# Layers 1 and 2 of a graph stack: rows gathered as plain fp32 and split on chip into two float32r pieces

## The chip, the cores and the metric

The kernel runs on one core of a Trainium2 chip. The metric is device time in microseconds (us) of the whole launch, as the median of several runs: 1704.35 us for the kernel before (three runs, 1702.13 to 1708.13). One more execution was taken by the hardware profiler; its times are those of the profile below. The engines are TensorE (PE, with its weight loads shown apart as PEld), VectorE (DVE), ScalarE (ACT), GpSimd (POOL) and SyncE (SP). Each runs its own instructions in order and waits on semaphores for the others.

## The reference

There are 3,327 nodes with 512 features each, and an adjacency matrix of 0 and 1 with some eight neighbours in the mean, but very many in the first rows. Four graph layers follow one another, each wrapped in a residual and a layer norm. What matters here are layers 1 and 2:

```python
# layer 1
mask = (adj > 0).astype(x.dtype)
deg = jnp.sum(mask, axis=1, keepdims=True)
agg = mask @ x / jnp.maximum(deg, 1.0)
self_f = x @ W_self + b_self
nb_f = agg @ W_nb + b_nb
out = relu(jnp.concatenate([self_f, nb_f], axis=-1) @ W_comb + b_comb)
x = layernorm(x + out)
# layer 2: the first 64 neighbours of each row are kept
nb_mean = keep @ x / jnp.maximum(cnt, 1.0)
out = leaky_relu(x @ W_line.T + b_line) + where(cnt > 0, leaky_relu(nb_mean @ W_nb.T + b_nb), 0)
x = layernorm(x + out)
```

Layers 0 and 3 are attention layers: every edge is weighted by a softmax over the row's neighbours, with 8 heads in layer 0 and 4 in layer 3.

## The kernel before

The nodes lie in 26 blocks of 128. From the adjacency matrix the kernel first makes, for every block, a list of its edges on chip (indices of the source rows and the place of the target row in the block), cut into chunks of 128 edges. Blocks 1 to 25 have 19 down to 5 chunks, 201 in all. Block 0, with the densest rows, is computed without a list: all 26 blocks of rows are read as they lie, and a 0/1 mask (`row0` in layer 1, `near0` in layer 2) takes the place of the selection.

Layers 1 and 2 share one routine, `mean_group` (L1452). The weights are applied first: the end of the layer before multiplies each block by the neighbour weights and stores the products in a table in DRAM, `t1_d` for layer 1 and `t2_d` for layer 2 (L727, L729). A row of a table holds three bf16 pieces of 512 values, whose sum is the fp32 value; `pieces` (L808) makes them with two ACT and two DVE instructions a block. `mean_group` works on groups of up to four chunks, in stages; at every `yield` it lets the other live groups and block ends go on:

1. `gather` (L962) takes slots of a ring in SBUF and issues on POOL one indirect DMA for each chunk (L966): 128 rows by index. For block 0 these are plain DMAs, also from POOL (L1460).
2. `select` (L975) has DVE compare the edge's place with the lane number. This gives a 128x128 matrix of 0 and 1 per chunk, in bf16 in layer 1; in layer 2 in fp8, into `sall`, which layer 3 uses again.
3. For every chunk PE multiplies the selection with the three pieces, three matmuls of 512 columns (L1474), all added up in one PSUM bank per block.

When a block's last group is done, its end is queued: `layer1_end` (L1512) and `layer2_end` (L1612) divide by the degree, add what the node itself gives, normalise, transpose the block, multiply it by the next layer's weights, and store the next table (L738, on SP). `layer0_end` (L1376) does the same at the end of layer 0 and fills `t1_d`. The function `both` (L1482) takes one step of every live group, oldest first, and then one step of every live block end, and is called once for every group; this order is how the instructions stand on each engine. It is written out by hand from L1430 on; the stages before may be put in another order.

The ring is laid out in two tiles, `gt` (22 x 528 fp32 columns, `RING`, L544) and `gx` (3,072 columns, `MORE`, L545), which hold 15 and 4 rows of 3,072 bytes. Layer 0 and layer 3 use the same tiles for their own rows. A gather waits until the matmuls that read its slots before are done. `first_block` in layer 3 (L1092) computes block 0 there, with four tiles `gd` of its own for the rows that it reads.

The loop of layer 1 adds, besides the groups, the products of the node's own rows (`self_part`, L1503, and `own_part`, L1539) as block ends, so that PE has them between the groups.

Of the kernel before, what the change touches and what calls it, by code (L numbers as in the profile page):

```python
# [8 lines left out]
F32 = mybir.dt.float32  # L9
BF16 = mybir.dt.bfloat16  # L10
FP8 = mybir.dt.float8e4
F32R = mybir.dt.float32r
# [6 lines left out]
ALU = mybir.AluOpType  # L19
# [524 lines left out]
RING = 22 * 528  # L544
MORE = 3072  # L545
RANGE = 60.0
# [75 lines left out]
def sparse_path(ctx, tc, flag_i, x, adj, l0_w, l0_a1, l0_a2, l1_w_self, l1_b_self, l1_w_nb, l1_b_nb,  # L622
# [103 lines left out]
    t0_d = dram.tile([ROWS, H0 * (OUT0 + 2)], F32, name="t0_d")  # L726
    t1_d = dram.tile([ROWS, 3 * D], BF16, name="t1_d")  # L727
    z1_d = dram.tile([NP, D], F32, name="z1_d")
    t2_d = dram.tile([ROWS, 3 * D], BF16, name="t2_d")  # L729
    t3_d = dram.tile([ROWS, H3 * (OUT3 + 2)], F32, name="t3_d")  # L730
# [252 lines left out]
    class Gat:  # L983
# [107 lines left out]

        def first_block(self, pool, ps, pacc, mp, none, done):  # L1092

# [13 lines left out]
            nc.scalar.copy(lone, pl[0:1, :P])  # L1107
            G = pool.tile([P, H, M], F32, name="gd", bufs=4)
            nc.sync.dma_start(G[0:1].rearrange("p h m -> p (h m)"), self.table[0:1, :])
# [6 lines left out]
            def unit(c):  # L1116
                m = LAST if c == NB - 1 else P
                G = pool.tile([P, H, M], F32, name="gd", bufs=4)
                nc.sync.dma_start(G[:m].rearrange("p h m -> p (h m)"), self.table[2 + c * P:2 + c * P + m, :])
# [124 lines left out]
    lay, listlay, wxlay = ExitStack(), ExitStack(), ExitStack()  # L1244
    rows = pool_in(ctx, "s_rows").tile([P, RING], F32, name="gt")
    big = pool_in(listlay, "l0big")
# [13 lines left out]
    with ExitStack() as pro:  # L1260
# [57 lines left out]
        def first_rows():  # L1318

            zeros16 = lent(3 * D, BF16)  # L1320
            nc.gpsimd.memset(zeros16, 0.0)
            zero = zeros16[0:1, :]
            for r in range(2):
# [128 lines left out]
    def mean_group(item, table, whole0, done, sall=None):  # L1452
        b, l, c0, g, at = item
        n = NB if b == 0 else chunks_of[b]
        if b == 0:
            G = ring.take(g)
            for c in range(g):
                m = LAST if c0 + c == NB - 1 else P
                r0 = 2 + (c0 + c) * P
                nc.gpsimd.dma_start(G[:m, c, :], table[r0:r0 + m, :])  # L1460
            S = whole0[:, c0:c0 + g, :]
            yield
        else:
            G = gather(ring, table, l, c0, g)
            yield
            S = select(sp, l.dst, c0, g, BF16, kept(sall, b, at, g))
        yield
        if at == 0:
            accs[b] = pacc.tile([P, D], F32, name="acc")
        for c in range(g):  # L1470

            m = LAST if b == 0 and c0 + c == NB - 1 else P if b == 0 or sall else l.places(c0 + c)
# [12 lines left out]

    ring = Ring(3 * D, rows.bitcast(BF16), extra.bitcast(BF16))
    mlay = ExitStack()
# [4 lines left out]
    with ExitStack() as lay:  # L1492
# [19 lines left out]
        def layer1_end(b, acc):  # L1512
# [63 lines left out]
    with ExitStack() as lay:  # L1576
# [57 lines left out]
        while work.live or ends.live:  # L1634
            both()
        assert not summed2
        g3.finish(fin, ps)
    mlay.close()

    with ExitStack() as lay:
        pools = (Ring(H3 * (OUT3 + 2), rows, extra), pool_in(lay, "l3s", 3),
                 pool_in(lay, "l3pa", 4, space=PSUM), pool_in(lay, "l3p1", 3, space=PSUM))
# [12 lines left out]
        def verdict():  # L1656
# [11 lines left out]
            for ls in lists:  # L1668
                for l in ls:
# [15 lines left out]
        units = g3.first_block(pool_in(lay, "l3d", 2), pools[3], pools[2], pool_in(lay, "l3pm", 1, space=PSUM),  # L1685
                               nl, layer3)
        dense = Stages()
# [60 lines left out]
```

## Time and profile before

| what | value |
|---|---|
| median of the runs | 1704.35 us |
| span of the profiled execution | 1704.1 us |
| PE busy | 1523.7 us (89%) |
| DVE busy | 1243.4 us (73%) |
| POOL busy | 911.9 us (54%) |
| ACT busy | 773.2 us (45%) |
| first and last matmul of `mean_group`, layer 1 | 650.5 and 1025.5 us |
| the same, layer 2 | 1031.7 and 1353.2 us |
| gathers by index (L966), all layers | 846 |
| DMA traffic | 410.17 MB, mean 241 GB/s |

The span is the time from the first to the last instruction of the one execution that was profiled; the page gives no other time for it. In the profile a group of instructions has its line of the code, engine and operation, the tiles that it writes and reads (out<-in), partitions x elements and type, and the count. Then come the time in which at least one of them ran, the mean of one in ns, and the idle time of the engine before them with what ended it. PE's instructions overlap, so the busy time over the count is what one of them costs in a row, and the mean is longer. POOL's busy time is the time that it takes to issue its DMAs; the transfers run on after it. An fp32 matmul stands in the trace as two instructions.

### The profile page before, as it was taken

Reading aid. Unit: us, or ns where it says so; the run is one execution under the profiler, and the core shown is the slowest. Engines: PE = TensorE matmul, PEld = TensorE weight load, DVE = VectorE, ACT = ScalarE, POOL = GpSimd, SP = SyncE. Lnnn points to the kernel's source line nnn. Section 1 sums busy time; section 2 is a strip of 40 time slices with the busy share of each in tenths; the row PEclk is TensorE's granted clock in tenths of the full one; section 3 lists DMA queues with packets and bytes.
Section 4 is the critical chain, followed back from the end, with each engine's and each line's share of the span. In section 5 each row is a group of like instructions: output and inputs, shape, how many; then the busy total and the mean of one; then the engine's idle time right before and its main releaser. Section 6 shows DMA issues by size and latency. Waiting matters only on the chain.

```text
span 1704.1 us, 25362 instructions
## 1 busy us (share of the span) xinstructions
PE 1523.7 (89%) x7947; PEld 981.5 (58%) x7947; DVE 1243.4 (73%) x3256; ACT 773.2 (45%) x2411; POOL 911.9 (54%) x1008
## 2 busy tenths in 40 slices
PE   5798958999999999999999999889989866998774
PEld 4565746777666664444444444446555545877653
DVE  8999988999998973124777884565434468798986
ACT  6557855667776764111111121122223222566664
POOL 2000067777666613646776552477777552677770
PEclk9999979999999999999999999999999987999997
DMA  8623687998775637978998776589999664677772
GB/s 300 233 100 107 207 288 237 313 309 266 258 231 176 179 90 282 317 237 272 341 328 296 246 241 241 204 279 317 318 312 322 234 227 157 189 230 224 227 220 74
DMA packets 121982, 410.17 MB, mean 241 GB/s; under 512 B 24768, under 2 KB 26304, under 8 KB 121838
## 3 DMA queue, kind: packets, MB, share of 16 engines
q0 software_dynamic: 69584, 286.13, 52.8%
q1 hardware_dynamic: 52254, 122.32, 20.4%
q8 instruction: 65, 1.06, 0.3%
q14 instruction: 79, 0.65, 0.1%
HBM read 360.34 MB, written 48.04 MB: 240 GB/s over the span
## 4 chain that ended last, share of the span: by engine, by line
PE 61%; DVE 16%; DMA 11%; ACT 6%; issue 3%; POOL 2%; SPq 0%; DVEq 0%; ACTq 0%; POOLq 0%
PE po L765 20%; PE acc L1196 15%; PE acc L1474 14%; DMA gt<-t_d,idx 7%; PE po L998 6%; PE pt L750 2%; DVE cand L877 2%; DVE gt L1188 2%; DMA gx<-t_d,idx 2%; POOL gt L966 2%; PE pg L1168 2%; DMA gd<-t_d 1%; DVE cand L891 1%; DVE sl L889 1%; ACT h L1213 1%
## 5 line engine op out<-in xcount | busy, mean ns | idle before, releaser
L966 POOL DMA_INDIRECT gt<-t_d,idx x739 | 742.1, 1004 | 578.9 <-DVE some L893 210.6
L1196 PE MATMUL acc<-gt,sel 128*128 128x264 f32 (+4 forms) x1656 | 413.7, 399 | 27.1 <-issue 20.1
L1196 PEld LDWEIGHTS acc<-gt,sel 128*128 128x128 f32 (+2 forms) x1656 | 311.4, 195 | 97.8 <-issue 42.9
L1188 DVE TENSOR_TENSOR gt<-gt,pg 128x1536 f32<-128x1536 f32 (+2 forms) x128 | 238.6, 1864 | 6.3 <-ACT gt L1181 2.9
L765 PE MATMUL po<-wn,xt 128*128 128x512 f32 x416 | 192.9, 607 | 3.8 <-ACT xt L753 3.8
L1474 PE MATMUL acc<-gt,sall 128*128 128x512 bf16 x489 | 117.3, 379 | 17.6 <-DMA gt<-t_d,idx 14.3
L765 PEld LDWEIGHTS po<-wn,xt 128*128 128x128 f32 x416 | 77.2, 193 | 89.4 <-issue 78.4
L966 POOL DMA_INDIRECT gx<-t_d,idx x107 | 107.6, 1006 | 38.6 <-issue 14.9
L877 DVE MAX8 cand<-val 128x8 f32<-128x832 uint16 (+38 forms) x259 | 125.7, 522 | 0.0
L1474 PEld LDWEIGHTS <-sall 128*128 128x128 fp8e4 x603 | 58.3, 97 | 98.4 <-issue 35.3
L1474 PE MATMUL acc<-gt,sel 128*128 128x512 bf16 (+3 forms) x486 | 113.3, 379 | 0.0
L998 PE MATMUL po<-gt,xt 128*128 128x268 f32 x416 | 106.0, 400 | 2.0 <-ACT xt L757 1.7
L1474 PEld LDWEIGHTS <-sel 128*128 128x128 bf16 (+3 forms) x603 | 57.9, 98 | 80.0 <-issue 22.7
L1156 ACT ACTIVATE far<-place,nmid 128x384 int16<-128x384 int16 (+3 forms) x137 | 86.9, 637 | 37.5 <-DVE ds L1160 34.5
L753 ACT COPY xt<-pt 128x512 f32<-128x512 f32 x86 | 50.8, 591 | 113.3 <-PE pt L750 113.2
L998 PE MATMUL po<-w,xt 128*128 128x262 f32 x416 | 96.2, 384 | 1.6 <-ACT xt L757 1.6
L765 PE MATMUL po<-wl,xt 128*128 128x512 f32 x208 | 94.0, 594 | 2.9 <-ACT xt L753 2.9
L765 PE MATMUL po<-wx,xt 128*128 128x512 f32 x208 | 94.3, 596 | 1.3 <-ACT xt L753 1.2
L750 PE MATMUL pt<-s_ident,xres 128*128 128x128 f32 x520 | 79.9, 277 | 17.4 <-DMA xres<-in_x_dram 16.6
L750 PEld LDWEIGHTS pt<-s_ident,xres 128*128 128x128 f32 x520 | 63.8, 143 | 46.2 <-issue 31.2
L1009 ACT COPY tg<-po 128x264 f32<-128x264 f32 (+1 forms) x104 | 39.9, 392 | 110.8 <-PE po L998 108.9
L849 ACT ACTIVATE m<-ab 128x1664 bf16<-128x1664 int32 x50 | 80.4, 1607 | 20.5 <-DMA ab<-in_adj_dram 15.6
(273 smaller groups left out, 2555.4 us busy)
## 6 DMA issues: line engine op xcount, KB each, us to landing
ab<-in_adj_dram SPq DMA_DIRECT2D x25, 832.0 KB
ab<-in_adj_dram SPq DMA_DIRECT2D x25, 831.5 KB
t_d<-t SPq DMA_DIRECT2D x50, 384.0 KB
gt<-t_d POOLq DMA_DIRECT2D x38, 384.0 KB, 7.8
gt<-t_d,idx POOLq DMA_INDIRECT x739, 4.8
t_d<-tg SPq DMA_DIRECT2D x25, 264.0 KB
t_d<-tg SPq DMA_DIRECT2D x25, 260.0 KB
gd<-t_d SPq DMA_DIRECT2D x25, 260.0 KB
```

Source lines behind the costliest of these rows:

```text
L750: nc.tensor.transpose(pt[:, c, :], src[:, c * P:(c + 1) * P], ident)
L753: nc.scalar.copy(xt, pt)
L765: nc.tensor.matmul(po, xt[:, c, :], w[:, c], start=c == 0, stop=c == DC - 1)
L849: nc.scalar.activation(m, ab[s], AF.Sign, accum_out=half[:, s, b:b + 1])
L877: nc.vector.max(out=top, in_=seg)
L966: nc.gpsimd.indirect_dma_start(out=t[:m, c, :], out_offset=None, in_=table[:, :], in_offset=bass.IndirectOffsetOnAxis(ap=l.idx[:m, c0 + c: ...
L998: nc.tensor.matmul(pw[s], xt[:, c, :], self.w[:, c, s, :], start=c == 0, stop=c == DC - 1)
L1009: nc.scalar.copy(tb[:, s * hh:(s + 1) * hh, :], by_head[:, :, 1:])
L1156: nc.scalar.activation(far[:, :g * P], place[:, c0 * P:(c0 + g) * P], AF.Abs, bias=l.nmid, scale=2.0)
L1188: nc.vector.tensor_mul(Gc[:, :, :OUT], Gc[:, :, :OUT], w[:, :g].rearrange("p c (h o) -> p (c h) o", o=1).to_broadcast([P, g * H, OUT]))
L1196: nc.tensor.matmul(accs[b][s], S[:m, c, :], G[:m, c, s * hh * M:(s + 1) * hh * M], start=at + c == 0, stop=at + c == chunks_of[b] - 1)
L1474: nc.tensor.matmul(accs[b], S[:m, c, :], G[:m, c, k * D:(k + 1) * D], start=at + c + k == 0, stop=k == 2 and at + c == n - 1)
```

## The change

The tables `t1_d` and `t2_d` hold plain fp32 rows, 2,048 bytes instead of 3,072. Where `pieces` made three bf16 pieces, layer 0's end copies the product from PSUM with one ACT instruction and stores it; layer 1's end stores its sum as it is. The split moves to the reader. `mean_group` has one stage more: ACT copies the gathered group into `hi`, a float32r tile (rounded), DVE subtracts `hi` from the gathered rows in place and leaves a float32r tile `lo`, and PE makes two matmuls for each chunk, with `hi` and `lo`. The selection is float32r too: in layer 1 DVE writes it so; in layer 2 DVE still writes fp8 into `sall`, and ACT converts it; for block 0 ACT converts the mask.

The buffers change with it. The ring of layers 1 and 2 is one tile `gm` on the place of `gt`, with 16 slots of 512 columns, and behind them the first of three `hi` tiles and the first of three selections. Two more `hi` tiles lie where `gx` lay and beside it. For layer 3 the place is given back as a new tile `gr`, and POOL fills it and `gx`, now 2,112 columns, with zeros. `first_block` takes its four row tiles from the second of the side tiles.

```diff
-MORE = 3072
+MEAN = 16
...
-    t1_d = dram.tile([ROWS, 3 * D], BF16, name="t1_d")
+    t1_d = dram.tile([ROWS, D], F32, name="t1_d")
...
-    t2_d = dram.tile([ROWS, 3 * D], BF16, name="t2_d")
+    t2_d = dram.tile([ROWS, D], F32, name="t2_d")
...
+            held = [t.rearrange("p (h m) -> p h m", m=M) for t in
+                    (room[:, q * H * M:(q + 1) * H * M] for q in range(GROUP))]
+            G = held[-1]
...
-                G = pool.tile([P, H, M], F32, name="gd", bufs=4)
+                G = held[c % GROUP]
...
         tb = fin.tile([P, D], F32, name="tb", bufs=2)
-        t3 = fin.tile([P, 3, D], BF16, name="t3", bufs=2)
-        for _ in pieces(t3, tb, times(ps, xt, wn)):
-            pass
-        store(t1_d, b, t3.rearrange("p s d -> p (s d)"), 2)
+        nc.scalar.copy(tb, times(ps, xt, wn))
+        store(t1_d, b, tb, 2)
...
-            extra = pool_in(ctx, "s_more").tile([P, MORE], F32, name="gx")
-            sp = pool_in(ctx, "s_sel", 3)
+            aside = pool_in(ctx, "s_more", 2)
+            for _ in range(2):
+                aside.tile([P, GROUP * H3 * (OUT3 + 2)], F32, name="gx", tag="aside")
+            sp = pool_in(ctx, "s_sel", 2)
...
-            S = whole0[:, c0:c0 + g, :]
-            yield
         else:
             G = gather(ring, table, l, c0, g)
-            yield
-            S = select(sp, l.dst, c0, g, BF16, kept(sall, b, at, g))
+        yield
+
+        S, hi = sels.pop(0), upper.pop(0)
+        sels.append(S)
+        upper.append(hi)
+        if b == 0:
+            nc.scalar.activation(S[:, :g], whole0[:, c0:c0 + g, :], AF.Identity)
+        elif sall is None:
+            nc.vector.tensor_tensor(S[:, :g], lane1[:, None, :].to_broadcast([P, g, P]),
+                                    l.dst[:, c0:c0 + g, None].to_broadcast([P, g, P]), ALU.is_equal)
+        else:
+            have = select(sp, l.dst, c0, g, BF16, kept(sall, b, at, g))
+            nc.scalar.activation(S[:, :g], have, AF.Identity)
+        nc.scalar.copy(hi[:, :g], G)
+        yield
+        lo = G.bitcast(F32R)
+        nc.vector.tensor_sub(lo, G, hi[:, :g].bitcast(F32))
         yield
...
-            for k in range(3):
-                nc.tensor.matmul(accs[b], S[:m, c, :], G[:m, c, k * D:(k + 1) * D],
-                                 start=at + c + k == 0, stop=k == 2 and at + c == n - 1)
+            m = l.places(c0 + c) if b else LAST if c0 + c == NB - 1 else P
+            for k, part in enumerate((hi, lo)):
+                nc.tensor.matmul(accs[b], S[:m, c, :], part[:m, c, :],
+                                 start=at + c + k == 0, stop=k == 1 and at + c == n - 1)
...
-    ring = Ring(3 * D, rows.bitcast(BF16), extra.bitcast(BF16))
+    gm = room.tile([P, RING], F32R, name="gm", tag="ring")
+    wide, narrow = GROUP * D, GROUP * P
+    ring = Ring(D, gm[:, :MEAN * D].bitcast(F32))
+    upper = [gm[:, MEAN * D:MEAN * D + wide]]
+    upper += [aside.tile([P, GROUP * H3 * (OUT3 + 2)], F32R, name="hi", tag="aside")[:, :wide] for _ in range(2)]
+    upper = [t.rearrange("p (c d) -> p c d", d=D) for t in upper]
+    sels = [gm[:, MEAN * D + wide:MEAN * D + wide + narrow].rearrange("p (c i) -> p c i", i=P)]
+    sels += [sp.tile([P, GROUP, P], F32R, name="selr") for _ in range(2)]
...
-            t3 = fin.tile([P, 3, D], BF16, name="t3")
...
-            yield from pieces(t3, tb)
-            store(t2_d, b, t3.rearrange("p s d -> p (s d)"), 2)
+            store(t2_d, b, tb, 2)
...
+        rows = room.tile([P, RING], F32, name="gr", tag="ring")
+        extra = [aside.tile([P, GROUP * H3 * (OUT3 + 2)], F32, name=name, tag="aside") for name in ("gx", "gd")]
+        for t in (rows, extra[0]):
+            nc.gpsimd.memset(t, 0.0)
         g3.finish(fin, ps)
```

More of the change, by code (lines that the diff above doesn't have):

```diff
@@ L1090, in factors, with first_block @@
             return wide
-        def first_block(self, pool, ps, pacc, mp, none, done):
+        def first_block(self, pool, ps, pacc, mp, none, done, room):
             H, OUT, M = self.H, self.OUT, self.M
@@ L1117, in unit @@
                 m = LAST if c == NB - 1 else P
-                G = pool.tile([P, H, M], F32, name="gd", bufs=4)
+                G = held[c % GROUP]
                 nc.sync.dma_start(G[:m].rearrange("p h m -> p (h m)"), self.table[2 + c * P:2 + c * P + m, :])
@@ L1244, in sparse_path @@
     lay, listlay, wxlay = ExitStack(), ExitStack(), ExitStack()
-    rows = pool_in(ctx, "s_rows").tile([P, RING], F32, name="gt")
+    room = pool_in(ctx, "s_rows")
+    rows = room.tile([P, RING], F32, name="gt", tag="ring")
     big = pool_in(listlay, "l0big")
@@ L1318, in first_rows @@
         def first_rows():
-            zeros16 = lent(3 * D, BF16)
-            nc.gpsimd.memset(zeros16, 0.0)
-            zero = zeros16[0:1, :]
+            blank = lent(D)
+            nc.gpsimd.memset(blank, 0.0)
+            zero = blank[0:1, :]
             for r in range(2):
@@ L1470, in mean_group @@
         for c in range(g):
-            m = LAST if b == 0 and c0 + c == NB - 1 else P if b == 0 or sall else l.places(c0 + c)
-            for k in range(3):
-                nc.tensor.matmul(accs[b], S[:m, c, :], G[:m, c, k * D:(k + 1) * D],
-                                 start=at + c + k == 0, stop=k == 2 and at + c == n - 1)
+            m = l.places(c0 + c) if b else LAST if c0 + c == NB - 1 else P
+            for k, part in enumerate((hi, lo)):
+                nc.tensor.matmul(accs[b], S[:m, c, :], part[:m, c, :],
+                                 start=at + c + k == 0, stop=k == 1 and at + c == n - 1)
         ring.done()
@@ L1641, in sparse_path @@
     with ExitStack() as lay:
-        pools = (Ring(H3 * (OUT3 + 2), rows, extra), pool_in(lay, "l3s", 3),
+        pools = (Ring(H3 * (OUT3 + 2), rows, extra[0]), pool_in(lay, "l3s", 3),
                  pool_in(lay, "l3pa", 4, space=PSUM), pool_in(lay, "l3p1", 3, space=PSUM))
@@ L1685, in sparse_path @@
         units = g3.first_block(pool_in(lay, "l3d", 2), pools[3], pools[2], pool_in(lay, "l3pm", 1, space=PSUM),
-                               nl, layer3)
+                               nl, layer3, extra[1])
         dense = Stages()
```

## The prediction

> **What bounds the kernel now.** I read the page's slices first, to cut the span at the stages; then the busy time in those stretches, the waits, the chain, the groups by shape and the timeline. These stretches carry layer 1 (642 to 1100 us), layer 2 (1100 to 1353) and, for comparison, the middle of layer 3:
>
> ```profile
> core 0: us, PE busy (x) PEld busy (x) DVE busy (x) ACT busy (x) POOL busy (x), PEclk, DMA share, GB/s
> ...
> 712.00:800.00 88.00, 88.00 (x318) 41.39 (x317) 28.06 (x55) 16.84 (x31) 45.66 (x48) 1.00 0.76 248
> 800.00:1025.00 225.00, 224.38 (x800) 102.35 (x799) 173.28 (x357) 41.20 (x80) 146.01 (x147) 1.00 0.87 293
> 1025.00:1100.00 75.00, 68.89 (x234) 32.76 (x232) 34.77 (x60) 13.55 (x29) 21.51 (x28) 1.00 0.56 202
> 1100.00:1353.00 253.00, 228.55 (x1062) 138.81 (x1063) 127.00 (x312) 66.24 (x326) 191.03 (x189) 1.00 0.91 310
> 1500.00:1600.00 100.00, 86.37 (x594) 71.05 (x593) 90.39 (x207) 63.25 (x188) 76.22 (x79) 1.00 0.78 226
> ```
>
> Layer 1 is PE's: it never rests from 712 to 1025. In layer 2 nothing looks full, but POOL starts 189 gathers in 253 us, 1.34 each. Its timeline shows why: 0.95 us per gather and a 0.30 us gap that no release shortens, a pitch of 1.254. Then 189 x 1.254 = 237, plus 11 us by which gathers (191.03 - 189 x 0.953) overran 0.953: 248 of 253. So POOL's issue bounds layer 2. The chain there names PE and landings; that is where each gather is awaited. Layer 3 gathers 2,112 bytes a row, not 3,072, at the same 0.95 and 1.25 us: fewer bytes won't shorten the pitch.
>
> Where the 11 us come from shows best in layer 0. The timeline (start, duration) of DVE and POOL:
>
> ```profile
> 415.87 1.02 DVE L859 TENSOR_TENSOR val<-m,code 128x1664 uint16<-128x1664 bf16 x1
> 416.80 0.69 DVE L817 TENSOR_TENSOR t<-tb,t 128x512 bf16<-128x512 f32 x1
> ...
> 416.31 2.00 POOL L966 DMA_INDIRECT gt<-t_d,idx  x1 [0.30 <-PE pg L1174]
> ...
> 409.59 1.74 DVE L1188 TENSOR_TENSOR gt<-gt,pg 128x1536 f32<-128x1536 f32 x1
> 409.90 0.95 POOL L966 DMA_INDIRECT gt<-t_d,idx  x1 [0.30 <-issue]
> ```
>
> The gather at 416.31 found L859, then L817, running; both read two SBUF tensors. It ended 0.82 after L817 did (417.49 to 418.31). The one at 409.90, inside L1188, which reads one SBUF tensor and one PSUM tensor, took its usual 0.95.
>
> Prices from the groups by shape (busy us, mean ns of one); the last line, on one line of the code, has shortest, median and longest:
>
> ```profile
> L765 PE MATMUL po<-wn,xt 128*128 128x512 f32 x416 | 192.9, 607 | 3.8 <-ACT xt L753 3.8
> L1196 PE MATMUL acc<-gt,sel 128*128 128x264 f32 x900 | 221.4, 394 | 0.0
> L1188 DVE TENSOR_TENSOR gt<-gt,pg 128x1536 f32<-128x1536 f32 x70 | 121.6, 1737 | 3.3 <-ACT gt L1181 2.6 <-ACT sel L1183 0.5
> L1188 DVE TENSOR_TENSOR gt<-gt,pg 128x2048 f32<-128x2048 f32 x45 | 102.4, 2275 | 2.4 <-ACT sel L1183 1.7 <-ACT gt L1181 0.3
> L849 ACT ACTIVATE m<-ab 128x1664 bf16<-128x1664 int32 x50 | 80.4, 1607 | 20.5 <-DMA ab<-in_adj_dram 15.6 <-DVE val L859 4.7
> ...
> L1327 POOL MEMSET gt<- x1: 301/301/301, 8.9 to 8.9; 128x256 f32 x1
> ```
>
> An fp32 matmul is two instructions of 0.464 us (26 x 4 x 2 matmuls, 416 rows).
>
> **What the Trainium skill says.** "SBUF — State Buffer", Who interferes with whom: a DVE instruction with two SBUF inputs contends with a GpSimd instruction that reads SBUF, since the second input takes the shared port. The trace agrees: the held gather took 2.00 us, not 0.95. "FP8 and Floating Point Precision", TensorE Precision Notes: reduced-precision fp32 reads four bytes and truncates, while true fp32 takes four passes. The 0.928 us per fp32 matmul against 0.228 to 0.239 for bf16 agrees with four; float32r itself occurs in no trace so far. "SBUF — State Buffer", A bandwidth-pool intuition that's wrong, gives PE's moving operand about 614 GB/s, at two bytes an element. Were that a limit on bytes, float32r's four would stream at half pace; no run here shows it, and it gives the upper bound below.
>
> **The change part by part.**
>
> *PE.* Each chunk has three bf16 matmuls now: 0.684 us in layer 1 (36.06 us for 158 from 712 to 800), 0.717 in layer 2 (143.93 for 602). It gets two float32r ones, unseen here. Low end 0.24: one pass, as two passes over 264 columns cost 0.246 with fp32 weights. High end 0.464: the same four-byte stream at an fp32 instruction's pace. I take 0.24, by the four-pass reading. A chunk is then 0.48: 0.204 saved in layer 1, 0.237 in layer 2. Stretches: 712 to 800, 53 chunks, -11 us of PE; 800 to 1025, 148, -30 (to 194); the two dense parts of layer 1, 26 each, -5 each; layer 2, 201, -48 (to 181).
>
> *DVE.* The loop that cuts the groups gives, followed through, 71 of them in layer 1 (its seven dense ones among them) and 65 in layer 2 (9 fragments at the ring's end, 38 of three chunks, 17 of four, one of one). A subtraction over three chunks is priced by L1188: 1.74; four, 2.28; two, 1.21; about 0.533 a chunk and 0.16 a group. Layer 2: +117, so 244. From 800 to 1025: 79 + 7 - 27 for the removed pairs (39 of 0.684) gives 232.
>
> *POOL.* Nothing is added to its program, but each subtraction reads G and hi, both SBUF. A gather that finds it running ends 0.82 after it, so loses the rest of it less 0.13. With a start each 1.254, the mean loss is D - 0.63 - 0.13: 1.0 us for three chunks, 1.5 for four, 0.5 for two. Layer 2: 38 x 1.0 + 17 x 1.53 + 9 x 0.48 = 68; for 189 of 201 gathers, 64. Bounds by phase: each subtraction just misses a start (27) or just beats one (102). I take 64, since landings scatter. The selection, directly behind, could hold the gather on, as L817 did: this is in the upper bound. Layer 2 becomes 248 + 64 + 5 = 317 against 253, say +65. From 800 to 1025: 136 starts x 1.254 = 171, plus 10 that gathers overrun already (140.0 us busy less 136 x 0.953), plus 46 (136/201 of 68): 227. 712 to 800, 48 starts: 60 + 16 = 76.
>
> *Layer 1 summed.* First part: -5 for PE; the new ring tile must wait for the last read of layer 0 (646 against a first load at 642.6), +3: -2. 712 to 800: PE and POOL near 77, with a little friction 79: -9. 800 to 1025: DVE 232, POOL 227, PE 194; three queues in a written order wait for each other, so I add 12, between none and 30: 245, +20. End: -5 for PE, +1 for a later last group: -4. Together +5.
>
> *ACT.* The copy to hi costs 1.48 for three chunks, by L849's 0.966 ns a column; S costs about 0.5. Layer 2: 66 + 99 + 33 = 198 of 317, hidden behind POOL. Without that cover, the stage would be DVE's 244 and still not ACT's.
>
> *Pieces at block ends.* Layer 0 sheds two DVE and one ACT instruction per block, 36 us of DVE over all 26, but its chain is mostly PE (393.66 busy of 412 from 230 to 642): -5, between 0 and -12. Stores fall from 384 to 256 KB; SP issues as many, 0.32 each.
>
> *Waits and buffers.* The ring has 16 slots for 19, with one stage more. Use of a slot: issue 4.1, landing about 4, S and hi 2, subtraction 1.7, matmuls 1.5, queues 5: 18 us. At 1.57 a gather 16 slots last 25; hidden, else a few us per block. hi and S rotate over three: ACT waits for the matmuls of three groups ago, with the transposed-block copies behind it, and PE's products behind those. PE is not the late engine then; cost 0, at worst one weight product (3.4) now and then. Draining costs hi and subtraction once more in layer 2: +3.
>
> *Layer 3.* POOL clears 13,728 columns: at most 16 us by L1327, from about 1353, where it idles 27.03 us until its first gather at 1375.52. Hidden; uncovered, 16. Its ring loses one slot of 27: +1.
>
> Sum: -5 + 5 + 65 + 3 + 1 = +69 on the profiled 1704.1 us: 1773. The runs' median is 0.25 above that span; I make no correction.
>
> **Rivals.**
>
> *Gathers aren't held, and it gets faster.* If subtractions start just after a gather has read its indices (they follow a landing, so phases may lock), layer 2 stays at 253, the larger of POOL's 248 and DVE's 244. Layer 1: -2 - 9 + 12 - 4 = -3, with less friction; layer 0 -8, drain +3, and -2 for PE's slack: 1694. For it: many single-block operations of 0.69 hold nothing. Against: a subtraction is longer than the pitch, so at three chunks and more a start always falls in it. It decides below about 0.15 us lost a group.
>
> *float32r runs at half that pace.* At 0.464, a layer 1 chunk costs 0.928, +0.244 x 253 = 62 us on a full PE: layer 1 takes 520 instead of 463. Layer 2's PE rises to 271, still under 317. Total 1773 + 57 = 1830. For it: the stated port rate; against: the four-pass reading.
>
> *The hold-up is partial.* At 27, with the same PE, layer 2 adds 28: 1736.
>
> **How the numbers follow.** Forecast 0.70, with its own range 1730 to 1830; partial hold-up (below that) 0.05; half pace 0.10; gathers free 0.15. The range 1705 to 1842 leaves out most of the faster rival and the far end of the slow one, about 2 in 10. Within 0.3% (5 us) a measurement can hardly tell from no change; of the faster rival's 0.15, 0.12 is below that band and 0.02 inside, so faster 0.12, same 0.03, slower 0.85.
>
> **What would show it.** Right: in layer 2, gathers near 1.3 us on average with gaps still 0.30, each long one under a subtraction; PE idle a third of the stage; the float32r matmul near 0.24 busy. Layer 1: DVE above 90% from 800 on, with PE waiting for it. Wrong: gathers at 0.95 with subtractions beside them; layer 2 at 253; float32r near 0.46; POOL waiting over 0.30 for accumulating matmuls (the ring); a first layer 3 gather later than 22 us after layer 2's last matmul.

## The result and the profile after

The changed kernel takes 1813.16 us (median, 1809.72 to 1815.97) where the kernel before took 1704.88 beside it: ratio 1.0626, 95% interval 1.0601 to 1.065. I had forecast 1773 with a range of 1705 to 1842, and slower with a chance of 0.85. The time lies in the range and on the forecast side, but the loss is half as large again as the sum of my steps, 106 us between the two profiled spans against 69. The page after begins:

```profile
span 1810.3 us, 25312 instructions
## 1 busy us (share of the span) xinstructions
PE 1510.1 (83%) x7493; PEld 1033.8 (57%) x7493; DVE 1447.8 (80%) x3297; ACT 973.8 (54%) x2551; POOL 1019.7 (56%) x1010
...
PEclk9999989999999999999999999699899878899998
```

DVE has 204 us more to do, ACT 201; POOL executes two more instructions in all, the clearings, and is 108 us busier: 96 by gathers by index that last longer, 12 by the clearings. Cut at the stages, by the first and last indexed gather of each layer in the two traces:

| stretch | before, us | after, us | difference | my step |
|---|---|---|---|---|
| to layer 0's last aggregation matmul | 646.0 | 653.0 | +7.0 | -5 |
| from there to layer 1's first gather | 37.9 | 46.8 | +8.9 | -2 |
| layer 1, first to last gather | 331.3 | 353.2 | +21.9 | +11 |
| from there to layer 2's first gather | 68.5 | 51.4 | -17.1 | -4 |
| layer 2, first to last gather | 263.4 | 333.0 | +69.6 | +65 |
| from there to layer 3's first gather | 28.4 | 44.2 | +15.8 | +3 |
| layer 3 to the end | 328.5 | 328.7 | +0.2 | +1 |

Busy time by stretch of the kernel after, core 0 (columns as in the table of before: PE, weight loads, DVE, ACT, POOL, clock, DMA). The first four rows are layer 1, the fifth is layer 2, the last the middle of layer 3:

```profile
core 0: us, PE busy (x) PEld busy (x) DVE busy (x) ACT busy (x) POOL busy (x), PEclk, DMA share, GB/s
686.00:760.00 74.00, 74.00 (x254) 42.46 (x253) 34.17 (x33) 38.23 (x47) 49.27 (x45) 1.00 0.70 215
760.00:860.00 100.00, 81.71 (x255) 46.61 (x254) 80.03 (x111) 36.05 (x35) 79.06 (x58) 0.95 0.60 179
860.00:1050.00 190.00, 165.75 (x502) 87.82 (x502) 175.76 (x284) 64.48 (x68) 133.77 (x108) 0.97 0.61 185
1050.00:1104.00 54.00, 50.43 (x163) 27.92 (x163) 43.27 (x61) 22.29 (x27) 17.20 (x30) 0.94 0.54 170
1104.00:1437.00 333.00, 243.29 (x905) 170.11 (x903) 247.56 (x387) 185.08 (x453) 246.45 (x201) 0.88 0.60 169
1606.00:1706.00 100.00, 85.91 (x585) 70.81 (x584) 89.38 (x205) 62.64 (x186) 76.23 (x79) 1.00 0.78 225
```

From 860 on DVE is the busiest engine of layer 1, at 92%. In layer 2 no engine is above 75%, and the gathers alone make POOL busy for 246 us where they took 202 before. The kernel before, from its first to its last gather of layer 2:

```profile
1084.00:1347.00 263.00, 235.81 (x1072) 140.57 (x1073) 132.34 (x320) 67.83 (x330) 202.17 (x200) 1.00 0.92 311
```

The timeline of after inside layer 2 (start, duration) has the hold-up that I forecast:

```profile
1262.44 2.29 DVE L1482 TENSOR_TENSOR gm<-gm 128x2048 fp32r<-128x2048 f32 x1 [1.25 <-ACT gm L1479]
...
1262.92 2.64 POOL L966 DMA_INDIRECT gm<-t_d,idx  x1 [0.30 <-PE acc L1490]
...
1264.65 0.55 DVE L978 TENSOR_TENSOR sall<-lane,dst 128x384 fp8e4<-128x384 bf16 x1
...
1267.11 0.94 POOL L966 DMA_INDIRECT gm<-t_d,idx  x1 [0.30 <-issue]
1267.52 1.76 DVE L1482 TENSOR_TENSOR gm<-gm,hi 128x1536 fp32r<-128x1536 f32 x1
1268.36 1.75 POOL L966 DMA_INDIRECT gm<-t_d,idx  x1 [0.30 <-issue]
```

The gather at 1262.92 found the subtraction running and ended at 1265.56, 0.83 after it; the one at 1268.36 ended at 1270.11, again 0.83 after. The one at 1267.11 had begun before the subtraction did and took 0.94. So it goes throughout: 59 gathers of layer 2 began inside a subtraction, and all of them ended 0.74 to 0.83 us after it. A selection that follows directly (1264.65), as it did in 58 of these cases, doesn't hold the gather on.

But that isn't all of it. A gather starts every 1.254 us where nothing is in the way, so layer 2's 200 intervals need 250.8. What lies above is either overrun (all that its gathers last beyond 0.953 us) or stall (the rest: POOL waiting with no gather running). Worked out so from each trace:

| layer 2 | first to last gather | overrun | stall |
|---|---|---|---|
| before | 263.4 | 13.0 | 0 |
| after | 333.0 | 57.2 | 25.0 |

The subtractions held the gathers for 44 us more, not 64, and POOL stood still for 25 us, where I had 5. The waits of layer 2 after (total us, times, longest us):

```profile
POOL gm L966 <- PE acc L1490: 50.0, 80, 13.9
ACT selr L1478 <- DVE sall L978: 45.2, 19, 12.1
DVE gm L1482 <- ACT hi L1479: 43.6, 33, 2.5
...
PE acc L1490 <- DVE gm L1482: 23.1, 22, 1.8
...
ACT gm L1478 <- DVE sall L978: 22.8, 11, 6.6
```

Read from the bottom up, this is a ring: ACT waits for DVE's selection before it casts it, and only then copies G to `hi`; DVE's subtraction waits for `hi`; PE waits for the subtraction; POOL waits for PE to give row slots back. Of POOL's 80 waits there, 24 us are the usual 0.30 after each gather; the other 26 are the stall.

The third finding lies between the layers, on the timeline of after:

```profile
1449.37 9.78 POOL L1661 MEMSET gr<- 128x11616 f32 x1 [11.02 <-PE acc L1490]
1449.93 0.69 DVE L1639 TENSOR_TENSOR e<-e,xres 128x512 f32<-128x512 f32 x1
...
1452.71 8.49 DVE L820 TENSOR_SCALAR xres<-e,mv,rs 128x512 f32<-128x512 f32 x1
...
1459.09 1.84 POOL L1661 MEMSET gx<- 128x2080 f32 x1
...
1461.26 1.12 PE L750 MATMUL pt<-s_ident,xres 128*128 128x128 f32 x4 [8.47 <-DVE xres L820]
```

DVE's scaling of the last block but one took 8.49 us, where it takes 0.55 elsewhere, and ended at 1461.20, just behind POOL's second clearing (1460.93). PE waited 8.47 us for it, with the rest of the way to layer 3 behind.

### The profile page after: what moved, and what is told of

Same layout as the page of the kernel before. It is cut to its first block, busy times and chain, and to the rows that moved or that the text cites. A ratio compares the mean times of both kernels' runs of the same rounds, so it can differ in the third digit from the quotient of the medians.

```text
span 1810.3 us, 25312 instructions
## 1 busy us (share of the span) xinstructions
PE 1510.1 (83%) x7493; PEld 1033.8 (57%) x7493; DVE 1447.8 (80%) x3297; ACT 973.8 (54%) x2551; POOL 1019.7 (56%) x1010
## 5 line engine op out<-in xcount | busy, mean ns | idle before, releaser
L966 POOL DMA_INDIRECT gm<-t_d,idx x402 | 506.7, 1260 | 169.8 <-PE acc L1490 94.9
L966 POOL DMA_INDIRECT gt<-t_d,idx x243 | 243.4, 1002 | 325.8 <-DMA ab<-in_adj_dram 211.9
L1482 DVE TENSOR_TENSOR gm<-gm,hi 128x1536 fp32r<-128x1536 f32 (+3 forms) x95 | 175.5, 1847 | 113.1 <-ACT hi L1479 112.9
L1198 PE MATMUL acc<-gt,sel 128*128 128x264 f32 (+2 forms) x972 | 241.7, 396 | 0.0
L966 POOL DMA_INDIRECT gr<-t_d,idx x173 | 169.3, 979 | 105.8 <-issue 32.3
L1198 PE MATMUL acc<-gr,sel 128*128 128x260 f32 (+3 forms) x692 | 177.6, 408 | 26.0 <-issue 18.3
L1479 ACT CAST hi<-gm 128x1536 fp32r<-128x1536 f32 (+3 forms) x95 | 146.0, 1540 | 75.1 <-DMA gm<-t_d,idx 64.8
L1198 PEld LDWEIGHTS acc<-gr,sel 128*128 128x128 f32 (+3 forms) x692 | 133.1, 200 | 52.6 <-issue 24.3
L1490 PE MATMUL acc<-hi,selr 128*128 128x512 f32 (+3 forms) x301 | 141.1, 469 | 9.7 <-ACT hi L1479 8.3
L1190 DVE TENSOR_TENSOR gt<-gt,pg 128x1536 f32<-128x1536 f32 (+3 forms) x75 | 140.6, 1875 | 5.9 <-ACT sel L1185 4.9
```

The lines of the kernel that those rows point to most:

```text
L966: nc.gpsimd.indirect_dma_start(out=t[:m, c, :], out_offset=None, in_=table[:, :], in_offset=bass.IndirectOffsetOnAxis(ap=l.idx[:m, c0 + c: ...
L1190: nc.vector.tensor_mul(Gc[:, :, :OUT], Gc[:, :, :OUT], w[:, :g].rearrange("p c (h o) -> p (c h) o", o=1).to_broadcast([P, g * H, OUT]))
L1198: nc.tensor.matmul(accs[b][s], S[:m, c, :], G[:m, c, s * hh * M:(s + 1) * hh * M], start=at + c == 0, stop=at + c == chunks_of[b] - 1)
L1479: nc.scalar.copy(hi[:, :g], G)
L1482: nc.vector.tensor_sub(lo, G, hi[:, :g].bitcast(F32))
L1490: nc.tensor.matmul(accs[b], S[:m, c, :], part[:m, c, :], start=at + c + k == 0, stop=k == 1 and at + c == n - 1)
```

## The experiments

My theory after the traces: in layer 2 two limits lie one just under the other, the held gathers and the ring of waits, and both come from the subtraction; the clearing between the layers adds 8 us. The rivals: DVE's added time alone, the shorter row ring alone, or the second matmul.

All ratios are to the kernel before beside the same runs (1706.85 to 1710.44 us, e9 to e11 apart).

### e1: an operation with one SBUF input in the subtraction's place

```diff
-        nc.scalar.copy(hi[:, :g], G)
+        nc.scalar.mul(hi[:, :g], G, 2.0 ** -9)
-        nc.vector.tensor_sub(lo, G, hi[:, :g].bitcast(F32))
+        with nc.allow_low_precision(reason='one input'):
+            nc.vector.tensor_reduce(lo, G[:, :, :, None], AX.X, ALU.add)
```

> The subtraction gives way to an operation of DVE that reads one SBUF tensor (a sum over an axis of length one), over the same columns in the same place; hi becomes G/512, so that the aggregate is G(1 + 1/512), not G. DVE, ACT, PE, the ring and the stages stay as in the changed kernel (1813.2 us). Theory (the second SBUF input holds POOL's gathers): layer 2, first to last gather 333 us, falls by the 48 to 65 us of overruns to 268 to 285, its gathers come back to about 1.0 us each; layer 1 gets back part of its 14 us; total 1733 to 1765. Rival (DVE's added load, or the extra stage and the short ring, hold POOL back through waits): as long an operation in the same place costs the same, layer 2 stays at 325 to 340, total 1805 to 1820.

Measured: 1778.39 us, ratio 1.0416 (1.0396 to 1.0436). Layer 2 took 314.7 us, between the two expectations. Groups and waits of its layer 2 (busy us, mean ns, then idle before):

```profile
L1483 DVE TENSOR_REDUCE gm<-gm 128x1536 fp32r<-128x1536 f32 (+3 forms) x63 | 112.0, 1778 | 52.9 <-ACT hi L1479 33.4 <-ACT gm L1479 12.6 <-DMA gm<-t_d,idx 6.8
...
L966 POOL DMA_INDIRECT gm<-t_d,idx x200 | 196.9, 985 | 117.8 <-PE acc L1491 82.2 <-issue 26.8 <-PE po L998 6.4
```

```profile
POOL gm L966 <- PE acc L1491: 82.2, 83, 18.0
```

The operation takes as long as the subtraction (1778 ns a time against 1771 and 1810), and yet a gather takes 985 ns, not 1232: overruns fall from 57.2 to 8.3. Counted from the traces, 79 gathers of layer 2 began inside this operation and overran by 1.1 us in all; the 59 that began inside the changed kernel's subtractions overran by 52.4. The edit also puts a sum in the place of a subtraction, so by itself it doesn't tell the second input from the kind of operation. The kernel before does: its L1188 has two inputs as well, one of them in PSUM, and the 133 gathers that began inside it took 0.95 us in the mean, none over 1.01. So it is the second SBUF input that holds them. In layer 1 the same edit takes 353.2 us back to 332.5. But in layer 2 the stalls rise from 25.0 to 55.6, so only 18 of the 49 us come out. Gathers that are free run into the ring of waits.

### e2: the subtraction chunk by chunk

```diff
-        nc.vector.tensor_sub(lo, G, hi[:, :g].bitcast(F32))
+        for c in range(g):
+            nc.vector.tensor_sub(lo[:, c, :], G[:, c, :], hi[:, c, :].bitcast(F32))
```

> The same subtraction, cut into one instruction per chunk of 512 columns (0.69 us each). Theory, if the port is let go between two instructions: a gather loses at most 0.1 us on each, the overruns of layer 2 fall from 48 us to 10 or less, layer 2 from 333 to about 290, total 1765 to 1780, since DVE pays some 0.15 us more per added instruction (about 270 of them, 40 us of DVE in all, on the path in layer 1 only). Theory, if a gather waits through a run of such instructions: layer 2 stays at 333 within 8, total 1810 to 1830. Rival (DVE's load sets the time): total 1825 to 1850, layer 2 longer than 333.

Measured: 1792.1 us, ratio 1.0487 (1.047 to 1.0505). Overruns in layer 2 are 13.0 us, as in the kernel before: a gather gets in between two instructions of a run, whose durations are 0.69. As in e1 the stage falls little, to 322.8, with 59.0 us of stalls; I had forecast 290.

### e5 and e6: the order on ACT and DVE, alone and together with e2

```diff
             G = gather(ring, table, l, c0, g)
+        have = select(sp, l.dst, c0, g, BF16, kept(sall, b, at, g)) if b and sall is not None else None
         yield
 
         S, hi = sels.pop(0), upper.pop(0)
+        nc.scalar.copy(hi[:, :g], G)
...
-            have = select(sp, l.dst, c0, g, BF16, kept(sall, b, at, g))
             nc.scalar.activation(S[:, :g], have, AF.Identity)
-        nc.scalar.copy(hi[:, :g], G)
```

> Only an order in the program changes: ACT copies G to hi before it casts S (after, S first), and in layer 2 DVE makes the selection one stage earlier, with the gathers. e1 left layer 2 at 315 us though its gathers were free again, with POOL waiting 82 us for accumulating matmuls; there ACT waits 70 us for the selection and DVE 46 us for hi. Theory (the gathers' hold-up and this ring of waits each set layer 2, one just under the other): with the hold-up still there POOL needs 201 x 1.254 + 57 = 309 us, so layer 2 falls from 333 to 309 to 325, total 1788 to 1808. Rival (the remainder is DVE's time or the length of the ring, not the order): 333 within 6, total 1805 to 1818.

Measured: 1805.96 us, ratio 1.0576 (1.0544 to 1.0608), which by the interval alone isn't parted from the changed kernel's 1.0626. The trace is: ACT's waits for the selection fall from 68.0 to 7.6 us, stalls from 25.0 to 9.2, and overruns rise from 57.2 to 65.2, since POOL now meets more subtractions. Layer 2 takes 325.2.

e6 has this order, the subtraction by chunks, and the clearing cut into 52 instructions:

```diff
-            nc.gpsimd.memset(t, 0.0)
+            for q in range(0, t.shape[1], 264):
+                nc.gpsimd.memset(t[:, q:min(q + 264, t.shape[1])], 0.0)
```

> Three edits together: the subtraction by chunks (as e2), the order of e5, and the clearing before layer 3 cut into 52 instructions of at most 264 columns, still on POOL. Theory for layer 2: hold-up gone and order mended, 270 to 295 us first to last gather (e2: 323; POOL's floor 201 x 1.254 = 252). Rival (ring or DVE's time): 310 to 323. Theory for the clearing (POOL holds the port for one instruction): DVE's scaling before layer 3 takes at most about 1 us in place of 8.49, and the 44.2 us between the layers fall to 31 to 36. Total 1730 to 1760 under the theories, 1775 to 1785 if only the clearing acts.

Measured: 1757.71 us, ratio 1.0284 (1.0238 to 1.0331). Layer 2 falls to 289.8, with overruns of 23.1 and stalls of 15.9. From the changed kernel's 333.0, the order alone gives 8 us, the chunks alone 10, both 43. That is what two limits look like of which the higher one counts. Waits of e6 in layer 2:

```profile
POOL gm L966 <- PE acc L1491: 37.2, 68, 6.6
ACT hi L1470 <- DMA gm<-t_d,idx: 25.9, 17, 2.8
```

ACT now waits first of all for landings, no longer for DVE. The clearing's part failed, and told more for it. The timeline of e6 behind layer 2:

```profile
1391.55 11.50 POOL L1663 MEMSET gr<- 128x264 f32 x44 [11.09 <-PE acc L1491]
1394.85 10.53 DVE L820 TENSOR_SCALAR xres<-e,mv,rs 128x512 f32<-128x512 f32 x1
...
1402.98 2.12 POOL L1663 MEMSET gx<- 128x264 f32 x8
```

52 instructions of 0.33 us each, and the scaling still ended only behind the last of them (1405.38 against 1405.10). A gather got in between the pieces of a subtraction on DVE, but DVE's scaling didn't get in between POOL's clearings, which stood queued one behind the other.

### e8: no subtraction, both matmuls kept

Left out is the subtraction; both matmuls read `hi`.

```diff
-        lo = G.bitcast(F32R)
-        nc.vector.tensor_sub(lo, G, hi[:, :g].bitcast(F32))
-            for k, part in enumerate((hi, lo)):
+            for k, part in enumerate((hi, hi)):
```

> Left out: the subtraction alone. Both matmuls of a chunk stay and both read hi, so that the aggregate is twice hi. All else as in the changed kernel. It parts PE's second matmul from DVE's subtraction, which e4 took out together. Theory (the subtraction, by hold-up and by its place in the ring of waits, makes the whole of layer 2's 70 us): layer 2 265 to 280 us, total 1690 to 1725, with layer 1 about 20 to 40 above e4's 282.5. Rival (the second matmul and the ring matter as well): layer 2 290 to 315, total above 1735.

Measured: 1693.12 us, ratio 0.9907 (0.9873 to 0.9942). Layer 2 takes 274.4 (overruns 14.4, stalls 9.2), layer 1 304.8, and the way from layer 0's last matmul to the first gather is back at 37.9. ACT's copies, the short ring, the further stage and the second matmul are all still there. So of the 69.6 us lost in layer 2, 58.6 are the subtraction's, and the kernel with all the rest of the change is 0.9% faster than before. Its layers 1 and 2, by first and last gather:

```profile
691.90:996.70 304.80, 301.26 (x999) 172.03 (x997) 173.46 (x365) 134.98 (x145) 200.07 (x202) 1.00 0.72 220
1047.50:1321.90 274.40, 225.85 (x904) 167.49 (x902) 137.26 (x323) 183.92 (x453) 203.45 (x200) 0.93 0.70 206
```

Set beside e1, whose operation takes as long as the subtraction, this splits the subtraction's cost:

| first to last gather, us | layer 1 | layer 2 | overrun in layer 2 | stall in layer 2 |
|---|---|---|---|---|
| e8, no subtraction | 304.8 | 274.4 | 14.4 | 9.2 |
| e1, one SBUF input | 332.5 | 314.7 | 8.3 | 55.6 |
| changed kernel | 353.2 | 333.0 | 57.2 | 25.0 |
| e6, by chunks, order mended | 336.5 | 289.8 | 23.1 | 15.9 |

In layer 1 the operation's time is worth 28 us and its second input 21; in layer 2 they are worth 40 and 18. With chunks and the other order layer 2 is within 15 us of e8, though DVE has all the subtractions to do. So the rival of DVE's added time alone can hold for no more than these 15 us there; in layer 1, whose order e5 hardly touches (352.2), it can hold for the whole 28.

### e4 and e7: without the lower piece

Left out are the subtraction and the second matmul, so that rows count to float32r only.

```diff
-        lo = G.bitcast(F32R)
-        nc.vector.tensor_sub(lo, G, hi[:, :g].bitcast(F32))
-            for k, part in enumerate((hi, lo)):
+            for k, part in enumerate((hi,)):
```

> Left out: the lower piece, that is the subtraction and the second matmul of each chunk, so that rows count to float32r only. All else as in the changed kernel: ACT's copy, the ring of 16, the stages. Theory: without the subtraction layer 2 is POOL's again, first to last gather 255 to 270 us, and layer 1 falls to what POOL and ACT need, some 20 to 60 us below the changed kernel; total 1670 to 1730. Rival (the ring and the longer chain of stages limit the gathers): layer 2 above 300.

Measured: 1664.15 us, ratio 0.9738 (0.9722 to 0.9755); layer 1 282.5, layer 2 271.3 us. A little better than forecast, for layer 1 fell by 71 us and not by 60 at most. Against e8 the second matmul is worth 22 us in layer 1, which PE fills, and 3 in layer 2.

e7 adds the order of e5 and the cut clearing.

> e4 (no lower piece: no subtraction, one matmul a chunk, so rows count to float32r only) with the order of e5 and the clearing of e6. Expected: layer 2 from 271 to 258 to 270 us (POOL's floor 252), the way from layer 2 to layer 3 from 39 to 28 to 33, layer 1 the same within 6; total 1640 to 1658. If the clearing holds DVE as before and the order does nothing: 1664 within 4.

Measured: 1661.09 us, ratio 0.9723 (0.9694 to 0.9751), not parted from e4. Layer 2 came to 266.5 as forecast; the way to layer 3 stayed at 42.9 us, with the scaling at 8.30, for the reason seen in e6.

### e3, e9, e10, e12: where the clearing lies

e3 has it on ACT (and, in layer 0, one copy on DVE in place of ACT):

```diff
-            nc.gpsimd.memset(t, 0.0)
+            nc.scalar.activation(t, ident[:, 0:1].to_broadcast([P, t.shape[1]]), AF.Identity, scale=0.0)
...
-        nc.scalar.copy(tb, times(ps, xt, wn))
+        nc.vector.tensor_copy(tb, times(ps, xt, wn))
```

> Two edits in stages that do not touch: the clearing between layers 2 and 3 goes from POOL to ACT, and in layer 0 the copy of the product out of PSUM goes from ACT to DVE. Theory for the first (POOL's memset held DVE's one-input operation, 8.49 us in place of 0.55): that operation is back at 0.55 us and the 44.2 us between layer 2's last gather and layer 3's first fall by about 8, to 36; if the memset only happened beside it, 44 within 2, or more, since ACT has 9 us more to do. Theory for the second (the copy waits in ACT's queue): layer 0's last aggregation matmul comes back from 653 to 646 us; otherwise 653 within 2. Total 1798 to 1806 with both or the first alone, 1813 or more with neither.

Measured: 1818.32 us, ratio 1.064 (1.0622 to 1.0658), no gain. Its timeline:

```profile
1461.58 0.55 DVE L820 TENSOR_SCALAR xres<-e,mv,rs 128x512 f32<-128x512 f32 x1
...
1472.28 9.89 ACT L1661 ACTIVATE gr<-s_ident 128x11616 f32<-128x11616 f32 x1
1482.06 1.94 ACT L1661 ACTIVATE gx<-s_ident 128x2080 f32<-128x2080 f32 x1
1483.89 0.57 ACT L1025 ACTIVATE mean<-pmean 1x512 f32<-1x512 f32 x1
```

The scaling is back at 0.55, and the matmul for the mean row starts 25.3 us after the last gather where it was 36.5: the clearing on POOL had cost 11 us. But on ACT it stands ahead of the copy of that mean row, which starts 12.0 us after its matmul where it was 3.7. The way between the layers is 40.3 for 44.2. The copy in layer 0 didn't help: layer 0's last matmul lies at 659.0, not 646. Of the 6 us beyond the changed kernel's 653.0, 2.7 were there at layer 0's first gather already (223.7 against 221.0).

e9 and e10 put the clearing on DVE, in e7's and in e6's kernel.

```diff
-            for q in range(0, t.shape[1], 264):
-                nc.gpsimd.memset(t[:, q:min(q + 264, t.shape[1])], 0.0)
+            nc.vector.memset(t, 0.0)
```

> e7 (no lower piece, the order of e5) with the clearing before layer 3 on DVE, in two instructions, in place of 52 on POOL. In e7 the 52 held DVE's scaling for 8.30 us, no better than the one long instruction did; on DVE nothing is on POOL to hold it, and the 13,696 columns come after the last scaling, where DVE waits some 6 us for the last transposed block. Theory: the scaling is back at 0.55 us, the way from layer 2 to layer 3 falls from 43 us by 8 less what of the clearing shows: 35 to 40 with a clearing of 7 us[...], 41 to 45 with 14; ratio to before 0.964 to 0.972 (e7: 0.9723). Layers 1 and 2 as in e7 within 4 us.

> e6 (both pieces, subtraction by chunks, the order of e5) with the clearing on DVE as in e9. There the scaling took 10.53 us. Theory: 0.55 us again, the way from layer 2 to layer 3 from 46.3 to 36 to 42, layers 1 and 2 as in e6 within 5; ratio to before 1.020 to 1.028 (e6: 1.0284), still slower than before, since DVE's subtractions remain.

These two and e11 ran on another chip, on which the kernel before took 1905.86 us and on which all four layers took longer in every kernel; neither their times nor their stages can be set beside the others. There e9 has a ratio of 0.9931 (0.9911 to 0.9951) and e10 1.0046 (1.0027 to 1.0065). What can be read is the order: the scaling takes 0.55 us, and the clearing 9.74 and 1.79 on DVE, ahead of the sums that the mean row needs, for which PE waited 7.05 us in e9 and 9.45 in e10. So the cost moved, as on ACT. For the sizes that I had named they are inconclusive.

e12 leaves it on POOL, in e7's kernel, behind one column of the last block's scaled rows:

```diff
-            for q in range(0, t.shape[1], 264):
-                nc.gpsimd.memset(t[:, q:min(q + 264, t.shape[1])], 0.0)
+        late_mark = fin.tile([P, 1], F32, name="late_mark")
+        nc.gpsimd.tensor_copy(late_mark, xres[item[0]][:, 0:1])
+            nc.gpsimd.memset(t, 0.0)
```

> e7 without its cut of the clearing: two long instructions on POOL as in the changed kernel, but behind a copy of one column of the last block's scaled rows, so that POOL can't begin them before DVE's last scaling is done. Theory (the clearing holds only what DVE runs beside it): both scalings of the last two blocks take 0.55 us; the clearing's 11.6 us lie beside the last block's matmuls and copies, and hold at most some small operations of DVE ahead of the table's first rows; the way from layer 2 to layer 3 falls from 42.9 us to 33 to 38, ratio to before 0.965 to 0.971 (e7: 0.9723). Rival (the clearing is in the way wherever it lies, as it was on ACT and DVE): 41 to 45, ratio 0.971 to 0.974.

Measured: 1653.98 us, ratio 0.9696 (0.9683 to 0.971). The timeline behind layer 2:

```profile
1307.98 0.55 DVE L820 TENSOR_SCALAR xres<-e,mv,rs 128x512 f32<-128x512 f32 x1
1308.67 0.18 POOL L1659 COPY late_mark<-xres 128x1 f32<-128x1 f32 x1 [17.92 <-DVE xres L820]
1309.11 9.78 POOL L1661 MEMSET gr<- 128x11616 f32 x1 [0.25 <-issue]
...
1316.53 0.26 DVE L1030 TENSOR_REDUCE mx<-g3fall 128x4 f32<-128x104 f32 x1 [3.30 <-ACT g3fall L1010]
...
1316.99 3.70 DVE L1032 TENSOR_SCALAR mx<-mx 128x4 f32<-128x4 f32 x1
...
1318.83 1.84 POOL L1661 MEMSET gx<- 128x2080 f32 x1
```

The same 11.6 us of clearing now lie beside the last block's matmuls. All that they hold are three small operations of four columns, which run beside each other, for 3.7 us. The way to layer 3 falls to 35.2 us, from e7's 42.9. The ratios alone hardly part the two, since their intervals touch; the traces do. This is the fastest kernel of the study, faster than the kernel before and the changed one, but it has no lower piece: it gives up the accuracy that the split is for.

### e11: the kernel before with a shorter ring

```diff
-    ring = Ring(3 * D, rows.bitcast(BF16), extra.bitcast(BF16))
+    ring = Ring(3 * D, rows.bitcast(BF16))
```

> The kernel before, with 15 row slots for layers 1 and 2 in place of 15 + 4, and nothing else changed: the ring alone. My prediction's step (the shorter ring is hidden): layer 2 stays at 263 within 4 us, layer 1 within 4, total within 0.3% of before. Rival (the ring's length is part of what layer 2 lost): layer 2 longer by 8 us or more, ratio 1.005 or above.

Measured, on that other chip: ratio 0.9992 (0.9975 to 1.001). There, four slots fewer cost nothing by themselves. In its layer 2 POOL waited 43.7 us for PE to give rows back, in waits of up to 6.3 us, where the kernel before, on the chip of its trace, waits for rows only in the usual 0.30 us; since that kernel has no trace on this chip, what the shorter ring would cost where nothing else is slower isn't shown. Whether the further stage and the ring together would, with no subtraction, is left to e8, which bounds them, with ACT's copies, at 11 us in layer 2.

## Why the prediction was right or wrong

Of the 37 us beyond the sum of my steps, layer 0 makes 12, the start of layer 1 11 and its middle 11, layer 2 5 and the stretch with the clearing 13; the end of layer 1 gives 13 back.

**PE, one float32r matmul at 0.24 us: right for matmuls in a row, too low as a mean.** Three of layer 2 after:

```profile
1261.38 0.39 PE L1490 MATMUL acc<-gm,selr 128*128 128x512 f32 x1
1261.61 0.39 PE L1490 MATMUL acc<-hi,selr 128*128 128x512 f32 x1
...
1261.84 0.40 PE L1490 MATMUL acc<-gm,selr 128*128 128x512 f32 x1
```

One starts every 0.23 us, in one instruction; the rival of half pace is out. The four-byte stream is no limit here. But many matmuls stood alone or ran at a lower clock, so that one was busy for 0.27 us from 686 to 760 and for 0.32 in layer 2. PE was busy there for 243 us of the 333, where I had 181; it wasn't the limit, and what this added to the waits for it isn't tested. That PE's saving is real shows best in e8's layer 1, which PE fills: 301 us of PE in place of 331. That is 30 us, where I had 41 in the stretches from 712 to 1025.

**DVE, 1.74 us for three chunks: right** (1.76, and 2.29 for four).

**POOL, 64 us by the hold-up: the mechanism right, the size nearly half too large.** Each hold ends some 0.82 after its subtraction, as I had read from layer 0. I had the subtractions fall anywhere in the pitch; they lost 0.82 us a time in layer 2 (mean over 64) where my mean over the sizes was 1.06, and overruns rose by 44. That lies between my 64 and the 27 of the rival of a partial hold-up, but no hold was partial. Of the 64 subtractions 5 met no gather, and the others met one 0.78 us after their start in the mean, where an even spread gives 0.63; why isn't shown. These holds make 52.4 us, where my mean loss gives 68, and all other gathers overran by 5 us, where the stage had 13 before. The selection directly behind, which I had let hold the gather on in the upper bound, didn't.

**Waits and buffers at nothing: the step that failed.** I had asked whether 16 slots last long enough on the average and whether PE is late. I hadn't asked what the two new instructions on ACT do to the order on DVE: `hi` stands behind the cast, the cast behind DVE's selection, and DVE's next subtraction behind `hi`. Layer 2 lost 25 us by it with the gathers held, and 56 with the gathers free (e1). The total of layer 2, 69.6 against 65, was right by luck, because the one error paid for the other. The rival of free gathers at 1694 would have failed on this too: e1 frees them and is at 1778.

**Layer 1, +5: too small.** Its start lost 8.9 where I had -2, and e8 shows that this too is the subtraction: without it the 37.9 us of before return. In the middle the loss was 21.9, where I had 11 and DVE as the limit. e8 and e1 show three parts of it: without the subtraction the middle is 26.5 us shorter than before, DVE's time puts 27.7 on again, and the hold-up, for which I had POOL's 227 us just under DVE's 232, another 20.7. The end gave 17.1 back where I had 4. e1 and e8 have that too (50.1 and 50.9 us for 51.4), so it isn't the subtraction's; 26 chunks save PE some 5 us, and what the rest is stays open.

**The clearing hidden by POOL's idle time: wrong.** POOL did idle; the work that it hindered was DVE's. The Trainium skill says so, and I had used one half of the same section: "SBUF — State Buffer", Who interferes with whom, has a fast form of DVE's copies and `tensor_scalar` operations take the port pair shared with GpSimd, so that whoever comes first blocks the other for its whole instruction. The trace agrees (8.49 us in place of 0.55). It also has an operation with two SBUF inputs collide only with a GpSimd instruction that reads, and a clearing only writes: L1639 took 0.69 beside it. The clearing itself took 11.6 us and not 16; it covers 13,696 columns, since `gx` has 2,080 and not 2,112, and 2,080 bytes is also what a row of layer 3 has. My signal for this step, a first gather of layer 3 more than 22 us after layer 2's last matmul, came at 33.

**The drain, +3:** from last gather to last matmul 6.1 became 11.5 us, so +5.

**Layer 3, +1: right** (+0.2).

**Layer 0, -5: wrong, and not settled.** It lost 7. DVE is relieved as I said, 211.0 us busy from 380 to 646 where it was 235.5, but PE, which never rested from 380 to 500 before, rests for 4.1 us in the first 40 of these. In this stage the written order may be changed, and a single copy moved to DVE (e3) made it 3 us longer still. That the order of instructions is the cause is likely from this, not shown.

## What to carry to other kernels

Before an operation is put where it reads two SBUF tensors beside a stream of gathers, or a POOL instruction beside DVE's scalings and copies, look up what each will hold, in both directions; one instruction per chunk let the gathers through here (overruns from 57 to 13 us) and cost little. When a stage is found bound by one thing, take that away in thought and ask for the next limit, with the order on each in-order queue: here the chunks took 44 us of overruns away, which was worth 10, and 43 once the order was mended too. A piece of work whose engine idles is hidden only if what it occupies is idle too.

## What the runs showed of the hardware that I had not expected

- A queue of 52 POOL clearings of 0.33 us held one DVE scaling as long as two of 9.78 and 1.84 us did (10.53, 8.30 and 8.49 us), until the last had ended. The section named above speaks of the whole instruction; here it was the whole queue. The other way round, a gather did get in between DVE's subtractions by chunk.
- Beside a clearing, DVE's sum over an axis (0.26 us) and its two-input sum (0.69) took their usual time; three operations of four columns each took 3.6 to 3.7.
- PE's granted clock in layer 2 was 1.00 of full speed in the kernel before, where PE was busy for 90% of the stage, 0.93 in e8 (82%) and 0.88 in the changed kernel (73%). In the stretch from 1297.3 to 1311.0 of after it was 0.50, and float32r matmuls in a row started every 0.43 us, not 0.23. At the end of layer 2, 16 matmuls of a block's product took 6.43 us just after PE had waited 2.37 us, and 3.69 where they followed other matmuls. No run tests this apart.
